# Strassen products for weights times values in the three graph-attention layers of layer 3

## The chip, the cores and the metric

The kernel runs on one core of a Trainium2 chip. The core has five engines, each with its own queue of instructions that it works off in order: TensorE (PE, matrix products into PSUM), VectorE (DVE), ScalarE (ACT), GpSimd (POOL) and SyncE (SP, which here only issues DMAs). Engines wait for each other through semaphores. The metric is the device time of one execution in microseconds (us); lower is better.

## What is computed

A graph of 3327 nodes with 256 features each goes through four residual blocks, `x = layernorm(x + layer(x, adj))`. Layers 0 to 2 are three kinds of masked attention over the adjacency matrix. Layer 3 is a stack of three graph-attention layers, called 3a, 3b and 3c in the kernel:

```python
def _gat_layer(h, adj, W, a):
    Wh = h @ W
    f1 = Wh @ a[:F_out]
    f2 = Wh @ a[F_out:]
    e = leaky_relu(f1 + f2.T, 0.01)
    att = softmax(where(adj > 0, e, NEG_INF), axis=1)
    return elu(att @ Wh)

h = input @ W0
h = _gat_layer(h, adj, W1, a1)
h = _gat_layer(h, adj, W2, a2)
h = _gat_layer(h, adj, W3, a3)
```

All of it is float32. The kernel multiplies the weights by the layer's input first and applies W afterwards (attention is linear in its values), so the large product has shape 3327 x 3327 x 256 in each of the six layers, and the projection is a small product of 256 x 256 per row.

## The kernel before

The nodes are padded to 26 tiles of 128. Queries are worked off in seven blocks: six of 512 queries (four tiles) and a last one of 256 (two tiles). `steps` runs over layers, blocks b and key tiles j; NB is 7 and NT is 26.

For each step `make_weights` builds one tile `e` of unnormalized weights, 128 keys by 512 queries. In the graph-attention layers (`Gat.weights`) that is one ACT instruction, `re` = relu(th * u - rh), and one DVE instruction, `e` = (re + rh) * mask. The vectors `th` and `rh` (one number per key, from `Gat.keys`) and `u` (one per query, from `Gat.block`) hold exponentials, shifted by maxima over all nodes that `Gat.shift` finds so that nothing overflows. The steps are made two to three ahead (LA = 2). There are five buffers for `e` and four for `re`.

PE then multiplies `e` by the values V (256 columns and one column of ones, whose sums norm the weights) into four PSUM banks, the `po` tiles: 257 columns per product, for each key tile and each query tile (L1562). V holds two generations, since the output of one layer is written while the input is read.

Layers 0 (inner blocks) and 2 use Strassen's method instead, over pairs of key tiles: a pair of weight tiles is a 2 x 2 block matrix (two halves of queries, two key tiles), a pair of value tiles another (two key tiles, two halves of features). Seven half-size products take the place of eight. `sums` adds the four combinations of weights (four DVE operations of 128 x 256 per pair, into `ssum`, tag acc with two buffers). `combine` makes the four combinations of values (DVE, once per pair and layer), which go to DRAM (`t_d`) and come back for each block through `fetch_tsum` (256.5 KB each, three buffers, issued on SP). `products` issues the 14 products per pair (L890); `joined` puts the seven results together at the end of a block, on DVE, with one ACT copy.

After a block, `finish` runs as a generator: one piece of it is advanced per step of the next block. In layer 3 before: norm the rows (L1133 to L1137), turn them by a DMA transpose (`turn`: two ACT copies into `planes`, the DMA, two DVE copies, L955), project by W (`projected4`, itself a Strassen product for blocks before the last two, with 12 DVE additions; a plain product, L1174, for the other blocks), elu (L1183, L1186, L1198), a running sum (L1036), and for 3a and 3b the scores of the next layer (L702, two per tile). In 3c the residual and the layer norm follow instead.

The first instructions stand in an order written out by hand (`manual_schedule`, until step 3); after that the framework's scheduler decides how the instructions of an engine follow each other, so the pieces of a finish are interleaved with the weights of the next block. Of tag x4k there are two buffers: the planes and turned rows of a finish, the combinations and, in layer 2, a block's queries (`gT`) share them.

```python
    def strassen(L, b):
        return L.key == "2" or (L.key == "0" and 0 < b < NB - 1)
```

The last block of 3c (`end`) is worked by a path of its own, with the weights kept in V.

Of the kernel before, what the change touches and what calls it, by code (L numbers as in the profile page):

```python
# [8 lines left out]
F32 = mybir.dt.float32  # L9
# [4 lines left out]
AF = mybir.ActivationFunctionType  # L14
ALU = mybir.AluOpType
AX = mybir.AxisListType
# [3 lines left out]
P = 128  # L20
# [4 lines left out]
ALPHA = 0.01  # L25
BETA = 1.0 - ALPHA
# [7 lines left out]
def gnn_stack(ctx: ExitStack, tc: tile.TileContext, a: dict, N: int, out: bass.AP):  # L34
# [8 lines left out]
    nc = tc.nc  # L43
    NT = (N + P - 1) // P
    NP = NT * P
    NB = (NP + CH - 1) // CH
# [36 lines left out]
    n = 8  # L83
# [9 lines left out]
    for k in range(4):  # L93
# [16 lines left out]

    t_d = {
        k: [dram.tile([P, 4 * H + 1], F32, name=f"t{k}_d{p}") for p in range(NT // 2)]
        for k in ("0", "2")
    }
    x_d = {
        k: [dram.tile([P, D], F32, name=f"x{k}_d{t}") for t in range(NT)]
# [478 lines left out]
    def by_pairs(L, b, p):  # L595
        return L.key == "2" and b < NB - 1 and p in (KPAIRS if b > 0 else (5, 7, 8, 10))
# [92 lines left out]
    class Gat:  # L689
# [23 lines left out]
        def shift(self, n):  # L713


            mx = cols.tile([P, 2], F32, tag="mx", name="mx")
            nc.vector.tensor_reduce(mx, self.sd[:, :, :n], AX.X, ALU.max)
            am = cols.tile([P, 2], F32, tag="am", name="am")
            nc.gpsimd.partition_all_reduce(am, mx, P, bass_isa.ReduceOp.max)

            self.nd = cols.tile([P, 1], F32, tag="nd", name="nd")
            self.nc = cols.tile([P, 1], F32, tag="ncs", name="ncs")
            self.ub = cols.tile([P, 1], F32, tag="ub", name="ub")
            nc.vector.tensor_scalar(self.nd, am[:, 1:2], -BETA, None, ALU.mult)
            nc.vector.tensor_tensor(self.nc, am[:, 0:1], am[:, 1:2], ALU.add)
            nc.vector.tensor_scalar(
                self.nc, self.nc, -BETA, 60.0, ALU.mult, ALU.add
            )
            nc.vector.tensor_scalar(self.nc, self.nc, 0.0, None, ALU.min)
            nc.vector.tensor_tensor(self.ub, self.nc, self.nd, ALU.subtract)  # L730

        def keys(self, lo, hi):
            d = self.sd[:, 1, lo:hi]
            nc.scalar.activation(self.th[:, lo:hi], d, AF.Exp, bias=self.nd)
            nc.scalar.activation(
                self.rh[:, lo:hi], d, AF.Exp, bias=self.nc, scale=ALPHA
            )
            nc.vector.tensor_scalar(
                self.nrh[:, lo:hi], self.rh[:, lo:hi], -1.0, None, ALU.mult
            )  # L740
# [10 lines left out]
        def block(self, b):  # L751

            wd = bw(b)
            u = work.tile([P, CH], F32, tag="u", name="u", bufs=2)
            nc.sync.dma_start(
                u[:, :wd], s_d[b].rearrange("o n -> (o n)").partition_broadcast(P)
            )
            for _ in range(6):
                yield
            nc.scalar.activation(  # L760
                u[:, :wd], u[:, :wd], AF.Exp, bias=self.ub, scale=BETA
            )
            self.u[b] = u

# [27 lines left out]


    def strassen(L, b):
        return L.key == "2" or (L.key == "0" and 0 < b < NB - 1)

    tsums = {}

    kept = {("0", 0): 1, ("0", 1): 1, ("0", 2): 1, ("2", NT // 2 - 1): 0}

    def combine(key, p, v, e=None):

# [242 lines left out]
    def finish(L, b, pos):  # L1045
# [5 lines left out]
        wd = bw(b)  # L1051
# [69 lines left out]
                    yield  # L1121
        else:
            p4 = work.tile([P, 4, D], F32, tag="stage", name="p4", bufs=4)
            if L.key == "2":
                z = joined(pos, b, p4)
                nc.vector.tensor_scalar(z, z, TINY, None, ALU.max)
                nc.vector.reciprocal(z, z)
                for k in range(n):
                    nc.scalar.mul(p4[:, k, :], p4[:, k, :], z[:, k : k + 1])
            else:  # L1130
                for k, t in enumerate(ts_):
                    ri = cols.tile([P, 1], F32, tag="ri", name="ri", bufs=4)
                    nc.vector.tensor_scalar(  # L1133
                        ri, pos[k][:, D : D + 1], TINY, None, ALU.max
                    )
                    nc.vector.reciprocal(ri, ri)
                    nc.scalar.mul(p4[:, k, :], pos[k][:, :D], ri)  # L1137
# [10 lines left out]
            if L.key != "2":  # L1148
                pT4 = work.tile([P, 4, 2, P], F32, tag="x4k", name="pT4", bufs=2)
                yield from turn(  # L1150
                    p4,
                    n,
                    lambda t: pT4[:, :n].bitcast(U16).rearrange(
                        "p k h (i t) -> p t k h i", t=2
                    )[:, t],
                    turn_steps(L, b),
                )
                pTs = {k: pT4[:, k] for k in range(n)}
                if b < NB - 2:
                    c4 = work.tile([P, 4, D], F32, tag="x4k", name="c4", bufs=2)  # L1160
                    yield from projected4(pT4, w[L.w], c4)

            def projected(k):


                if L.key == "2":
                    src = p4[:, k, :]
                elif b < NB - 2:
                    src = c4[:, k, :]
                else:  # L1170
                    pm = bank("pproj")
                    pT = pTs.pop(k)
                    for h in range(2):
                        nc.tensor.matmul(  # L1174
                            pm[:, :D],
                            pT[:, h, :],
                            w[L.w][:, h, :],
                            start=(h == 0),
                            stop=(h == 1),
                        )  # L1180
                    src = pm[:, :D]
                e = work.tile([P, D], F32, tag="elu_e", name="elu_e", bufs=2)
                nc.scalar.activation(e, src, AF.Exp)  # L1183
                if L.hidden:
                    y = work.tile([P, D], F32, tag="y", name="z", bufs=6)
                    nc.vector.tensor_scalar(y, src, 0.0, -1.0, ALU.max, ALU.add)  # L1186
                else:
                    y = work.tile([P, D], F32, tag="y", name="y", bufs=6)
                    nc.vector.scalar_tensor_tensor(
                        y, src, 0.0, xr[k], ALU.max, ALU.add  # L1190
                    )
                es[k] = e
                ys.append(y)
# [10 lines left out]
            for p in range(n + 2):  # L1204
                if p >= 2:
                    activated(p - 2)
                    if b == NB - 2:
                        yield
                if 1 <= p <= n:
                    projected(p - 1)  # L1210
                if p > 0:
                    yield
        if not L.hidden:
# [54 lines left out]
            for k in range(0, n, 2):  # L1268
                follow((k, k + 1), dsts)
                yield  # L1270
        if L.gat_next is not None:
            if b == NB - 2:
                yield
                L.gat_next.shift(ts_[-1] + 1)
                yield
                L.gat_next.keys(0, ts_[-1] + 1)
                yield
                if L.key == "0":
                    yield
                    yield  # L1280
            else:
                for _ in range(3):
                    yield
            L.gat_next.rows(b)
        if b == NB - 1:
            for t, x in L.late:
                yield
                L.sum.add(t, x)
            yield
            L.sum.close(nxt[NT - 1])  # L1290
            if L.key == "1":
                yield
                combine("2", NT // 2 - 1, nxt)
            if L.gat_next is not None:
                L.gat_next.keys(ts_[0], NT)

# [126 lines left out]
    def make_weights(L, b, j):  # L1423
        if strassen(L, b) and j % 2 == 0 and kept.get((L.key, j // 2)) != b:
            fetch_tsum(L.key, b, j // 2)
        if L.is_gat:
            made.append(L.gat.weights(b, j))
        elif by_pairs(L, b, j // 2):
            made.append(next(pairs[b, j - j % 2]))
            if j % 2:  # L1430
                e1, e2 = made.pop(), made.pop()
                made.append(None)
                made.append(sums(b, e1, e2))
        else:
            made.append((weights0 if L.key == "0" else weights2)(b, j))
            if strassen(L, b) and j % 2:
                e2, e1 = made.pop(), made.pop()
                made.append(None)
                made.append(sums(b, e1, e2))
# [37 lines left out]
    for s, (L, b, j) in enumerate(steps):  # L1477
# [120 lines left out]
        if nb == NB:  # L1598
            nl, nb = (None if last else layers[L.i + 1]), 0
        begin = 2 if last and b == NB - 2 else 14  # L1600
        if L.is_gat and (b, j) == (0, 22):
            sum_weights(w[L.w])
        if L.key == "2" and b * NT + j in KSTEPS:
            sum_keys(KSTEPS[b * NT + j])
# [90 lines left out]
```

## Time and profile before

| | |
|---|---|
| device time, three runs | 2330.83, 2332.19, 2332.12 us (median 2332.12) |
| span of the profiled execution | 2330.8 us |
| mean granted TensorE clock | 0.998 |
| instructions | 34802 |
| DMA | 214.77 MB, mean 92 GB/s |

The profiled execution is one run; its span is from the first to the last instruction, and equals the shortest of the three times to the precision shown, so little lies around it. In the page's row for DMA queues the one that SP feeds carries 212.28 MB and is busy 28.9% of sixteen engines' time.

By stretches of time (busy us of each engine), layer 2 and then three parts of layer 3:

```profile
900.00:1240.00 340.00, 340.00 (x2125) 288.85 (x2124) 296.74 (x898) 100.87 (x186) 0.00 (x0) 1.00 0.23 71
1735.00:1880.00 145.00, 145.00 (x710) 127.15 (x710) 95.14 (x225) 79.13 (x118) 0.00 (x0) 1.00 0.17 52
2050.00:2195.00 145.00, 145.00 (x708) 127.43 (x708) 96.99 (x232) 78.96 (x115) 0.00 (x0) 1.00 0.23 74
```

The columns are the stretch, its length, then PE, PE's weight loads, DVE, ACT and POOL with their counts of instructions, the granted clock, the DMA share and GB/s. PE is busy without a gap in all; DVE is busy 87% of the time in layer 2 and 66% in layer 3.

### The profile page before, as it was taken

To read this page: it belongs to the slowest core of one execution; us is meant where nothing else is said; L and a number is where in the kernel's file an instruction comes from. 1 tells how busy PE (TensorE), PEld (TensorE's weight loads), DVE (VectorE), ACT (ScalarE), POOL (GpSimd) and SP (SyncE) were. 2 spreads that over 40 slices of the span, in tenths; PEclk is the share of its full clock that TensorE was granted. 3 is DMA by queue.
4 is the path that set the end of the run, shared out by engine and by line. 5 is a ranking of instruction groups with operands and counts; after the bars stand their busy time and mean duration, and the time that the engine had idled before them with its cause. 6 is when DMAs were issued, how large, how long until landed. Compare 5 with 4: busy or idle time off the path is not lost.

```text
span 2330.8 us, 34802 instructions
## 1 busy us (share of the span) xinstructions
PE 2315.7 (99%) x12551; PEld 1975.3 (85%) x12551; DVE 1767.6 (76%) x4877; ACT 1207.5 (52%) x1923; POOL 38.8 (2%) x156
## 2 busy tenths in 40 slices
PE   9999999999999999999999999999999999999997
PEld 7788887888888778888888988888888888888887
DVE  7789999867777778889889876666656666666676
ACT  4677777765555422233323355555655555655553
POOL 0000001000000000000000000000000000000000
PEclk9999999999999999999999999999999999999999
DMA  8655565422222322213212321210211111132111
GB/s 278 192 188 183 173 193 188 150 82 80 75 70 72 100 55 89 80 46 93 75 51 83 107 84 55 70 52 27 77 48 44 46 58 53 44 100 70 62 45 46
DMA packets 147297, 214.77 MB, mean 92 GB/s; under 512 B 76093, under 2 KB 101172, under 8 KB 142516
## 3 DMA queue, kind: packets, MB, share of 16 engines
q1 hardware_dynamic: 146852, 212.28, 28.9%
q8 instruction: 99, 1.62, 0.3%
q14 instruction: 74, 0.61, 0.1%
q10 hardware_dynamic: 272, 0.26, 0.0%
HBM read 167.53 MB, written 28.19 MB: 84 GB/s over the span
## 4 chain that ended last, share of the span: by engine, by line
PE 98%; DVE 1%; DMA 0%; ACT 0%; issue 0%; SPq 0%; DVEq 0%; ACTq 0%
PE po L1562 52%; PE po L890 20%; PE ps L635 6%; PE ps L499 6%; PE ps L674 5%; PE pproj L1001 3%; PE po L1527 1%; PE pv L1255 1%; PE pgq L529 1%; PE pproj L1174 1%; PE pk L359 0%; PE pq L323 0%; DMA stage<-in_adj_a 0%; PE pn L335 0%; PE pr L175 0%; PE turned L80 0%
## 5 line engine op out<-in xcount | busy, mean ns | idle before, releaser
L1562 PE MATMUL po<-v,e 128*128 128x257 f32 x5616 | 1247.7, 381 | 0.1
L1562 PEld LDWEIGHTS po<-v,e 128*128 128x128 f32 x5616 | 1058.0, 190 | 163.2 <-issue 9.3
L768 ACT ACTIVATE re<-u,nrh,th 128x512 f32<-128x512 f32 (+1 forms) x728 | 555.7, 780 | 493.9 <-DVE e L779 488.4
L779 DVE SCALAR_TENSOR_TENSOR e<-re,rh,mask 128x512 f32<-128x512 f32 (+1 forms) x702 | 501.9, 718 | 340.4 <-PE po L1562 314.7
L890 PE MATMUL po<-tsums,ssum 128*128 128x128 f32 (+1 forms) x1794 | 250.5, 275 | 0.0
L890 PEld LDWEIGHTS po<-tsums,ssum 128*128 128x128 f32 x1794 | 225.5, 192 | 1.1 <-ACT y L1093 0.3
L890 PEld LDWEIGHTS po<-v,e 128*128 128x128 f32 x1196 | 172.7, 191 | 37.6 <-issue 24.1
L890 PE MATMUL po<-v,e 128*128 128x129 f32 x1196 | 185.9, 275 | 0.0
L512 ACT ACTIVATE ex<-ps,rq 128x512 f32<-128x512 f32 (+1 forms) x183 | 118.9, 652 | 115.2 <-PE ps L499 112.4
L484 DVE SCALAR_TENSOR_TENSOR e<-ex,mask 128x512 f32<-128x512 f32 (+1 forms) x182 | 115.6, 650 | 48.3 <-ACT ex L648 24.8
L513 DVE SCALAR_TENSOR_TENSOR e<-ex,mask 128x512 f32<-128x512 f32 (+1 forms) x183 | 117.2, 646 | 33.4 <-ACT ex L512 32.9
L499 PE MATMUL ps<-ft,ft 128*128 128x512 f32 (+1 forms) x312 | 142.5, 561 | 0.0
L648 ACT ACTIVATE ex<-ex,off 128x512 f32<-128x512 f32 x98 | 67.5, 717 | 132.0 <-DVE ex L664 94.4
L674 PE MATMUL ps<-gT,ft 128*128 128x512 f32 (+1 forms) x336 | 129.8, 527 | 0.0
L455 DVE CUSTOM_DVE_ANT_0 acc<-acc,stage 128x1024 uint16<-128x1024 uint16 (+1 forms) x168 | 109.0, 649 | 11.7 <-DMA stage<-in_adj_a 8.6
L682 ACT ACTIVATE ex<-ps,off 128x512 f32<-128x512 f32 (+1 forms) x84 | 51.8, 620 | 101.3 <-PE ps L674 100.1
L674 PEld LDWEIGHTS ps<-gT,ft 128*128 128x128 f32 x336 | 61.2, 190 | 44.5 <-issue 38.5
L890 PE MATMUL po<-tsums,e 128*128 128x128 f32 x598 | 92.2, 275 | 0.4 <-DVE c L1100 0.4
L890 PE MATMUL po<-v,ssum 128*128 128x128 f32 x598 | 92.3, 275 | 0.0
L442 ACT ACTIVATE mask<-pos 128x1024 uint8<-128x1024 bf16 (+1 forms) x87 | 86.4, 993 | 2.1
L441 ACT ACTIVATE pos<-stage 128x1024 bf16<-128x1024 int32 (+1 forms) x87 | 85.6, 983 | 0.0
L890 PEld LDWEIGHTS po<-tsums,e 128*128 128x128 f32 x598 | 79.3, 192 | 0.6 <-issue 0.6
(322 smaller groups left out, 2432.6 us busy)
## 6 DMA issues: line engine op xcount, KB each, us to landing
mask<-mask_d SPq DMA_DIRECT2D x30, 1664.0 KB
stage<-in_adj_a SPq DMA_DIRECT2D x78, 512.0 KB
tsums<-t_d SPq DMA_DIRECT2D x152, 256.5 KB
mask_d<-mask SPq DMA_DIRECT2D x6, 1664.0 KB
u<-s_d SPq DMA_DIRECT2D x24, 256.0 KB
xT<-in_xT SPq DMA_DIRECT2D x10, 512.0 KB
mask<-mask_d SPq DMA_DIRECT2D x5, 832.0 KB
t_d<-tsums SPq DMA_DIRECT2D x14, 256.5 KB
```

What stands on the lines that cost most here:

```text
L442: nc.scalar.activation(mask(b, j, 2), t_[:, : 2 * wd], AF.Sign)
L455: nc.vector.tensor_tensor(acc, acc, st[:, h * wd : (h + 1) * wd], ALU.add)
L484: nc.vector.scalar_tensor_tensor(e[:, :wd], t_[:, :wd], 0.0, mask(b, j), ALU.add, ALU.mult)
L499: nc.tensor.matmul(ps[:, :wd], FT[j // 4][:, 0, (j % 4) * P : (j % 4 + 1) * P], FT[b][:, 1, :wd], start=True, stop=True,)
L512: nc.scalar.activation(t_[:, c], ps[:, c], AF.Exp, scale=rq[:, j : j + 1])
L513: nc.vector.scalar_tensor_tensor(e[:, c], t_[:, c], 0.0, mask(b, j)[:, c], ALU.add, ALU.mult)
L635: nc.tensor.matmul(ps[:, i * D : (i + 1) * D], l, r, start=True, stop=True)
L674: nc.tensor.matmul(ps[:, :wd], FT[j // 4][:, h, (j % 4) * P : (j % 4 + 1) * P], g[:, h, :wd], start=(h == 0), stop=(h == 1),)
L768: nc.scalar.activation(t_[:, :wd], self.u[b][:, :wd], AF.Relu, bias=self.nrh[:, j : j + 1], scale=self.th[:, j : j + 1],)
L779: nc.vector.scalar_tensor_tensor(e[:, :wd], t_[:, :wd], self.rh[:, j : j + 1], mask(b, j), ALU.add, ALU.mult,)
L890: nc.tensor.matmul(o, x, y, start=(p == 0 and g not in banks[:i]), stop=(p == NT // 2 - 1 and g not in banks[i + 1 :]),)
L1562: nc.tensor.matmul(pos[k], e[:, k * P : (k + 1) * P], V[L.i % 2][i], start=(i == 0), stop=(i == NT - 1),)
```

## The change

Layer 3 takes the Strassen path: 3a and 3b in all seven blocks, 3c in all but the last. The combinations of values for it are made in the finish of the layer before (two pairs per block, the last pair at the end of the layer) and written to three new sets of DRAM tiles. The finish of a block in layer 3 begins with `joined`. The projection in layer 3 becomes plain in all blocks; layer 1 keeps the Strassen one. The weights of a graph-attention layer (layer 1 too) are shifted per query instead of by one common maximum, so that sums and differences of them stay in range; `shift` finds the minimum of the query scores beside the maximum of the key scores for that.

```diff
     t_d = {
         k: [dram.tile([P, 4 * H + 1], F32, name=f"t{k}_d{p}") for p in range(NT // 2)]
-        for k in ("0", "2")
+        for k in ("0", "2", "3a", "3b", "3c")
     }
...
             nc.vector.tensor_reduce(mx, self.sd[:, :, :n], AX.X, ALU.max)
+            lo = cols.tile([P, 1], F32, tag="lo", name="lo")
+            nc.vector.tensor_reduce(lo, self.sd[:, 0, :n], AX.X, ALU.min)
+            nc.vector.tensor_scalar(mx[:, 0:1], lo, -1.0, None, ALU.mult)
...
-            nc.vector.tensor_scalar(self.nd, am[:, 1:2], -BETA, None, ALU.mult)
-            nc.vector.tensor_tensor(self.nc, am[:, 0:1], am[:, 1:2], ALU.add)
-            nc.vector.tensor_scalar(
-                self.nc, self.nc, -BETA, 60.0, ALU.mult, ALU.add
-            )
-            nc.vector.tensor_scalar(self.nc, self.nc, 0.0, None, ALU.min)
-            nc.vector.tensor_tensor(self.ub, self.nc, self.nd, ALU.subtract)
+            nc.vector.tensor_tensor(self.nc, am[:, 1:2], am[:, 0:1], ALU.subtract)
+            nc.vector.tensor_scalar(self.nc, self.nc, BETA, 0.0, ALU.mult, ALU.min)
+            nc.vector.tensor_tensor(self.nc, self.nc, am[:, 1:2], ALU.subtract)
+            nc.vector.tensor_scalar(self.nc, self.nc, 60.0, None, ALU.add)
+            nc.vector.tensor_scalar(self.ub, am[:, 0:1], -BETA, None, ALU.mult)
+            nc.vector.tensor_tensor(self.nd, self.nc, self.ub, ALU.subtract)
...
     def strassen(L, b):
-        return L.key == "2" or (L.key == "0" and 0 < b < NB - 1)
+        if L.key == "0":
+            return 0 < b < NB - 1
+        if L.key == "3c":
+            return b < NB - 1
+        return L.key != "1"
...
-    kept = {("0", 0): 1, ("0", 1): 1, ("0", 2): 1, ("2", NT // 2 - 1): 0}
+    kept = {("0", 0): 1, ("0", 1): 1, ("0", 2): 1}
+    kept.update({(key, NT // 2 - 1): 0 for key in ("2", "3a", "3b", "3c")})
...
-            if L.key == "2":
+            if strassen(L, b):
                 z = joined(pos, b, p4)
...
-                if b < NB - 2:
+                if L.key == "1" and b < NB - 2:
                     c4 = work.tile([P, 4, D], F32, tag="x4k", name="c4", bufs=2)
                     yield from projected4(pT4, w[L.w], c4)
...
+                    if L.hidden and p % 2 and b < NB - 1:
+                        combine(layers[L.i + 1].key, (ts_[0] + p - 3) // 2, nxt)
...
             for k in range(0, n, 2):
                 follow((k, k + 1), dsts)
                 yield
+                if L.key == "2" and b < NB - 1:
+                    combine("3a", (ts_[0] + k) // 2, nxt)
...
-            if L.key == "1":
+            if L.i:
                 yield
-                combine("2", NT // 2 - 1, nxt)
+                combine(layers[L.i + 1].key, NT // 2 - 1, nxt)
...
-        if L.is_gat:
-            made.append(L.gat.weights(b, j))
-        elif by_pairs(L, b, j // 2):
+        if by_pairs(L, b, j // 2):
...
-            made.append((weights0 if L.key == "0" else weights2)(b, j))
+            if L.is_gat:
+                made.append(L.gat.weights(b, j))
+            else:
+                made.append((weights0 if L.key == "0" else weights2)(b, j))
             if strassen(L, b) and j % 2:
...
-        if L.is_gat and (b, j) == (0, 22):
+        if L.key == "1" and (b, j) == (0, 22):
             sum_weights(w[L.w])
```

The arguments of the exponentials in `Gat.keys` and `Gat.block` change with the shift (which of them has the factor 0.01, and a sign); their number stays.

## The prediction

> **What bounds the kernel now.** I read the page's busy times first, then the chain of waits, then the groups of instructions in layer 3, then the timeline of the vector engine (DVE). Page, busy times:
>
> ```profile
> PE 2315.7 (99%) x12551; PEld 1975.3 (85%) x12551; DVE 1767.6 (76%) x4877; ACT 1207.5 (52%) x1923; POOL 38.8 (2%) x156
> PE 98%; DVE 1%; DMA 0%; ACT 0%; issue 0%; SPq 0%; DVEq 0%; ACTq 0%
> ```
>
> TensorE is full, and the chain that ended last (second line) is 98% PE. The chain between 1720 and 1880 us shows one whole block of layer 3:
>
> ```profile
> 1767.46 26.22 PE po L1562 x120
> 1793.68 1.78 PE pproj L1001 x16
> 1795.46 1.74 PE po L1562 x8
> 1797.20 0.89 PE pproj L1001 x8
> 1798.09 1.74 PE po L1562 x8
> 1799.83 0.44 PE pproj L1001 x4
> 1800.27 15.60 PE po L1562 x72
> 1815.87 0.11 PE psr L746
> ```
>
> These sum to 48.5 us per block with no gap. A float32 matmul shows as two records; of 257 columns a record takes 15.60/72 = 216.7 ns. What Strassen's products take is in the chain of layers 0 and 2, where one pair of key tiles is 28 records, 3.12 us:
>
> ```profile
> 1241.79 3.12 PE po L890 x28
> ```
>
> Groups by form, 1735 to 1880 us (three blocks), then 900 to 1240 us (layer 2):
>
> ```profile
> L779 DVE SCALAR_TENSOR_TENSOR e<-re,rh,mask 128x512 f32<-128x512 f32 x78 | 58.2, 750 | 45.1 <-PE po L1562 42.0 <-PE psr L746 2.9
> L955 DVE COPY pT<-turned 128x1024 uint16<-128x1024 uint16 x6 | 4.1, 741 | 0.0
> ...
> L841 DVE TENSOR_TENSOR ssum<-e,ssum 128x256 f32<-128x256 f32 x52 | 21.9, 422 | 0.4
> ```
>
> In layer 3 the DVE waits for PE before its masks (45.1 of 145 us). That idle time is the room for the new work. The timeline of the DVE, 1005 to 1008 us, shows what an operation really occupies:
>
> ```profile
> 1005.86 0.42 DVE L840 TENSOR_TENSOR ssum<-ssum,e 128x256 f32<-128x256 f32 x1
> 1006.20 0.42 DVE L655 TENSOR_TENSOR ex<-ex,ps 128x256 f32<-128x256 f32 x1
> 1006.53 0.42 DVE L841 TENSOR_TENSOR ssum<-e,ssum 128x256 f32<-128x256 f32 x1
> 1006.86 0.42 DVE L656 TENSOR_TENSOR ex<-ex,ps 128x256 f32<-128x256 f32 x1
> ```
>
> It lasts 0.42 us but the next starts after 0.335. I price by these start-to-start steps wherever the DVE is never idle: 0.335 for 128x256, 0.20 for 128x128 (0.28 to 0.29 long), 0.662 for a layer-3 mask of 512 (0.75 long), 0.395 for one of 256, 0.345 for a score (L702), 0.64 for a turned copy, 0.08 for a column. Busy shares, which add up the long durations, overstate DVE load.
>
> **What the Trainium skill says.** "Perfetto Trace Analysis", section Identifying the Most-Contended Engine, warns that matmul busy share does not show how near PE is to its limit; here the chain, gapless and 98% PE, settles it. "VectorE: DVE Perf Modes", section The perf-mode tier table: `tensor_tensor` on float32 runs in the 1× mode, one element a cycle; at the page's 0.96 GHz that is 267 ns for 256; the trace agrees with 335 (68 fixed). Section The DRAIN you can't avoid says the next operation waits until the pipe is empty; the trace differs, overlapping 85 of 420 ns, and decides. "TensorE: Matmul & The Clock Gate", section What's actually happening: an idle window of about 3.4 us halves PE's clock. PE is never idle so long here (granted clock 0.998), so no run shows it.
>
> **The change, part by part.**
>
> *PE, removed.* A pair of key tiles was 16 records, 3.467 us; it becomes 28 records, 3.12 us: 0.347 less. Of a whole block's 13 pairs: 4.5 us. The half block (last, two query tiles) goes from 13 x 1.733 to 13 x 1.56: 2.25. There are 18 whole blocks (3a, 3b and 3c have six each), and two half blocks that change: 81.2 + 4.5 = 85.7 us. *PE, added.* Plain projections: 16 records of 256 columns, 3.47, for 28 of 128, 3.12: 0.35 more in 15 blocks, 5.2. Net on PE: -80.5 us, a whole block 44.1 instead of 48.5.
>
> *DVE, added and removed, per whole block of 3a or 3b,* counted in the instruction list of the changed program: 26 masks x 0.662 = 17.2; sums, 52 x 0.335 = 17.4 (new); joining the products, 2.9 (new, in place of eight columns, 0.6); turned copies 1.3; relu, elu and mean, 12 x 0.335 = 4.0; scores 8 x 0.345 = 2.8; combinations of values for the next layer, 8 x 0.20 = 1.6 (new). The 12 additions of the Strassen projection (4.0) go; relu now reads PSUM, 0.335 for 0.205. Sum 47.2, before about 29.5. So **DVE passes PE: 47.2 against 44.1**. In 3c, with no scores or combinations but with the layer norm: 44.3. Half block: 33.7 (it carries the finish of the whole block before) against 23.8 on PE. First blocks: 43.6 in 3a (PE 40.6), 41.7 in 3b and 3c (PE 42.3).
>
> *How it falls within a block.* With two sum buffers (tag acc) the DVE starts pair k's sums only when PE has done pair k-2, so it can be about 2.5 us ahead, no more. A plain pair is 2.66 us on DVE and 3.12 on PE: it gains 0.46 per pair. The list has two bursts: at the second pair the joining (6.2 us of DVE for one pair of PE work), and at the sixth and seventh relu, scores and combinations (together 13.4 to 13.7 us, against two pairs and the projections on PE, 9.7). The first uses up the lead (2.5 + 3.1 - 6.2: about 0.6 unhidden); the four pairs after it give back about 0.8, so of the second burst's 3.8 about 3.1 stay open; the six last pairs restore the lead. Whole block of 3a, 3b: 44.1 + 3.7 = 47.8. In 3c the second burst is smaller (5.4 to 5.8 and 2.9, then 3.1 and 4.7): 44.1 + about 0.7.
>
> *Waits that come with it.* The turn chain (scaled rows, planes, DMA transpose, pT) starts after the joining. From its last operation: four scalings 1.9, one `re` 0.8, two plane copies 2.0, the transpose 3.66 (the chain of waits shows DMA turned<-planes so once, at 776.95): 8.4 us; in the list the DVE has 7 masks and 10 sums before pT, 8.0. So about 0.4 us of wait a block, bounded below by 0 (PE-paced stretch) and above by 1.5 (on SP the transpose stands behind a fetch of combined values that waits for PE). Behind the waiting pT copies stand the next sums and masks, for which PE waits. The new fetches (256.5 KB a pair) go out when PE has done pair k-3 and are needed two pairs, 6.2 us, later; a fetch of layer 2 lands some 2.3 us after its issue, so I cost them at nothing; behind the 1664 KB mask the cover is 9 us against about 7. Combining for 3a in layer 2 adds 1.6 us of DVE to blocks of 85.5 us where PE is the limit: 0, at most 1 a block. The new shift is a few columns per layer: 0. Semaphore hops between ACT, DVE and PE: I take 0.6 a block in 3c, where slack is thin.
>
> *Sum.* 3a and 3b, ten whole blocks: 47.8 + 0.4 against 48.5: -3. 3c, five: 44.8 + 0.4 + 0.6 = 45.8: -13.5. Half blocks: 33.7 less the lead of 2.5 = 31.2 against about 29.5 (the starts of their finishing rows): +3.4. First blocks: +1 each in 3b and 3c (the tail of the half block's finish), 0 in 3a: +2. The tail: the fifth block of 3c now joins before it turns, 2.3 late: +2.3. Total about -8.8. The profiled span is 2330.8 us; the median of the runs shown, 2332.1, is 1.3 above, and the lowest is equal to the span. 2330.8 - 8.8 + 1.3 = **2323 us**. Of 80 us taken from PE, 72 are given to the DVE.
>
> **The rivals.**
> - *PE stays the limit:* the DVE's new work fits in its idle time. For it: 45 of 145 us idle before the masks. Against: 47.2 over 44.1, and a lead of one pair. 2332 - 80 = 2252 us. Chance 0.06.
> - *The turn chain decides (slower):* the DVE, now the limiting engine, stands at the pT copies for the DMA transpose. Price: each 0.4 us in 17 blocks is 7 us. From 0.9 us of wait a block the gain is gone; at the bound of 1.5 it is +19 on the forecast, 2342; own range 2337 to 2360. For it: 8.4 against 8.0, and PE-dependent fetches ahead of the transpose on SP. Against: the stretch before pT has no other finishing work, so part of the wait falls on DVE time that PE's pace leaves free. Chance 0.30.
> - *PE's clock drops:* gaps in PE add up to an idle window, and 3.4 us at half clock cost 1.7 in each of 17 blocks: 2353. Against: the open 3.1 us come in pieces between single products. Chance 0.05.
> - *Layer 2 gives it back:* the second combination of a block waits for the first one's DMA, since the query block holds the other buffer of tag x4k; 1 us in six blocks: 2330. Chance 0.10.
>
> **How the numbers follow.** The forecast has 0.49, own range 2310 to 2334. A measurement here tells 0.2%, 4.7 us. Faster by more: 0.43 of the forecast's case, plus 0.06: 0.49. Within: 0.06 of it, 0.09 of the layer 2 case, 0.05 of the turn case: 0.20. Slower: 0.31. The range to hold eight in ten: low 2300 (DVE steps 1% shorter and leads fully used), high 2350 (the upper bound of the turn wait and some of the others).
>
> **What would show it.** Right: PE busy falls in layer 3 and its idle time is put down to DVE e and ssum; DVE is near full there; whole blocks take about 48 us in 3a and 3b and 46 in 3c; the chain of waits alternates PE and DVE. Wrong: blocks of 44 us (PE still the limit), of 50 and more with DVE idle before pT on turned<-planes (turn chain), or a granted clock below 0.99.

## The result, and the profile after

The changed kernel takes 2340.9 us (median of five, 2337.6 to 2344.2) against 2331.9 (2330.8 to 2332.2) for the kernel before: ratio 1.004, 95% interval 1.0027 to 1.0052. It is slower by 0.4%, where 2323 and a gain were forecast. The profiled execution spans 2339.1 us, before 2330.8. (Its own time is 2340.9. In every run here whose span is on record the time lies 1.7 to 2.2 us above it, so some 2 us do lie around a span, before too.) The page's busy times and its DVE row of slices:

```profile
PE 2274.8 (97%) x15335; PEld 2017.4 (86%) x15335; DVE 2072.2 (89%) x6032; ACT 1206.9 (52%) x1928; POOL 53.2 (2%) x195
...
DVE  7789999867777778899889899999999999999997
```

PE's busy time fell by 41 us, and the DVE row is nines from the 24th slice to the last but one: the vector engine is full through layer 3. The chain of waits breaks off in this trace (its shares add up to 18% of the span), so I read windows. Columns are PE, PEld, DVE, ACT and POOL busy, the granted clock, the DMA share and GB/s. One whole block of 3b and one of 3c, before:

```profile
1730.50:1779.00 48.50, 48.50 (x239) 42.53 (x237) 31.73 (x76) 26.50 (x40) 0.00 (x0) 1.00 0.17 52
2095.20:2143.60 48.40, 48.40 (x237) 42.54 (x236) 32.38 (x78) 26.39 (x39) 0.00 (x0) 1.00 0.23 73
```

and after, with the half blocks of 3a and 3b (third and fourth line):

```profile
1738.00:1786.00 48.00, 44.30 (x374) 43.11 (x373) 47.10 (x126) 27.25 (x40) 1.34 (x2) 1.00 0.46 140
2110.00:2157.00 47.00, 45.48 (x384) 44.47 (x384) 45.39 (x127) 26.09 (x38) 0.00 (x0) 1.00 0.52 150
...
1660.00:1695.80 35.80, 31.15 (x205) 27.46 (x204) 33.16 (x133) 22.03 (x42) 0.71 (x3) 0.95 0.63 181
...
1979.80:2017.80 38.00, 31.89 (x214) 28.19 (x215) 33.24 (x133) 22.45 (x41) 0.71 (x3) 0.96 0.59 173
```

In the whole blocks PE went from never idle to 3.7 us (3b) and 1.5 us (3c) idle, while DVE went from two thirds busy to full: the limit has changed engines, as forecast. The half blocks are where the two kernels part most. Cutting the span at the first row scaling on ACT (p<-p,zs after, p<-po,ri before) of each block's finish gives the whole account:

| stretch | before | after | forecast change | measured |
|---|---|---|---|---|
| layer 2, up to its half block's finish | 466.1 | 468.5 | 0 | +2.4 |
| first block of 3a, and the tail | 42.0 + 41.0 | 45.8 + 38.9 | +2.3 | +1.7 |
| 3a, five whole blocks | 243.2 | 240.3 | -1.5 | -2.9 |
| half block of 3a, first of 3b | 74.2 | 81.3 | +2.7 | +7.1 |
| 3b, five whole blocks | 242.2 | 238.6 | -1.5 | -3.6 |
| half block of 3b, first of 3c | 74.2 | 83.1 | +2.7 | +8.9 |
| 3c, five whole blocks | 242.6 | 237.3 | -13.5 | -5.3 |

The sum is +8.4 (before rounding) where -8.8 was forecast (layers 0 and 1 differ by 0.1). The miss of 17.2 us lies in the half blocks (10.6 over the forecast), in 3c (8.2) and in layer 2 (2.4). The whole blocks of 3a and 3b did 3.5 better, and the first block of 3a with the tail 0.6. (These two share a row because the first scaling comes later in a block that is joined first.)

What ends a half block shows in the waits of the one in 3b, 1979.8 to 2017.8 (engine, line, what it waited for: us in total, times, longest):

```profile
PE po L897 <- DVE ssum L847: 2.7, 2, 2.3
DVE zs L929 <- ACT p L923: 2.7, 1, 2.7
ACT u L762 <- DMA u<-s_d: 2.6, 1, 2.6
...
PE po L897 <- DMA tsums<-t3b_d: 1.6, 2, 1.4
```

and in the timeline of DVE and ACT there (start, length, engine, line, operation; in brackets the idle time before it):

```profile
2008.29 0.28 DVE L846 TENSOR_TENSOR ssum<-e 128x128 f32<-128x128 f32 x1
...
2010.13 0.72 ACT L762 ACTIVATE u<-u,ub 128x512 f32<-128x512 f32 x1 [2.56 <-DMA u<-s_d]
...
2010.96 0.24 ACT L923 COPY p<-po 128x128 f32<-128x128 f32 x1
...
2011.24 0.16 DVE L929 COPY zs<-po 128x1 f32<-128x1 f32 x1 [2.66 <-ACT p L923]
2011.31 0.28 DVE L847 TENSOR_TENSOR ssum<-ssum,e 128x128 f32<-128x128 f32 x1
```

At the end of the block the DVE stands 2.66 us at the joining. Its row-sum copy (`zs`) starts when ACT's copy of M1 (the first of the seven products, `p<-po`) is out of PSUM, and that copy stands behind the exponential of a `u` of the next layer, for whose DMA ACT waits 2.56 us. Behind the waiting `zs` stand the block's own last two sums, for which PE waits 2.3 us. In 3a's half block the same hole is 2.05 us.

### The profile page after: what moved, and what is told of

It is laid out like the page before. It is cut to its first block, busy times and chain, and to the rows that moved or that the text cites. A ratio compares the mean times of both kernels' runs of the same rounds, so it can differ in the third digit from the quotient of the medians.

```text
span 2339.1 us, 42193 instructions
## 1 busy us (share of the span) xinstructions
PE 2274.8 (97%) x15335; PEld 2017.4 (86%) x15335; DVE 2072.2 (89%) x6032; ACT 1206.9 (52%) x1928; POOL 53.2 (2%) x195
## 5 line engine op out<-in xcount | busy, mean ns | idle before, releaser
L897 PE MATMUL po<-tsums,ssum 128*128 128x128 f32 (+1 forms) x4758 | 677.8, 278 | 13.9 <-DVE ssum L847 5.1
L897 PEld LDWEIGHTS po<-tsums,ssum 128*128 128x128 f32 x4758 | 605.3, 193 | 24.1 <-DVE ssum L847 7.6
L897 PE MATMUL po<-v,e 128*128 128x129 f32 x3172 | 503.1, 278 | 16.4 <-DVE e L781 15.1
L897 PEld LDWEIGHTS po<-v,e 128*128 128x128 f32 x3172 | 440.2, 192 | 64.0 <-issue 25.6
L1574 PE MATMUL po<-v,e 128*128 128x257 f32 x1664 | 376.0, 381 | 0.1
L1574 PEld LDWEIGHTS po<-v,e 128*128 128x128 f32 x1664 | 313.9, 190 | 53.9 <-issue 9.3
L897 PE MATMUL po<-tsums,e 128*128 128x128 f32 x1586 | 248.4, 276 | 0.0
L897 PEld LDWEIGHTS po<-v,ssum 128*128 128x128 f32 x1586 | 210.7, 192 | 1.2 <-DVE ssum L848 0.8
L845 DVE TENSOR_TENSOR ssum<-e 128x256 f32<-128x256 f32 (+1 forms) x416 | 167.4, 403 | 4.4 <-PE po L897 1.8
L848 DVE TENSOR_TENSOR ssum<-e,ssum 128x256 f32<-128x256 f32 (+1 forms) x416 | 168.1, 404 | 1.5
L847 DVE TENSOR_TENSOR ssum<-ssum,e 128x256 f32<-128x256 f32 (+1 forms) x416 | 167.7, 403 | 1.4
L846 DVE TENSOR_TENSOR ssum<-e 128x256 f32<-128x256 f32 (+1 forms) x416 | 167.5, 403 | 0.5
```

Of the source, the lines that this page charges most:

```text
L845: nc.vector.tensor_tensor(s3, e11, e21, ALU.subtract)
L846: nc.vector.tensor_tensor(s1, e21, e22, ALU.add)
L847: nc.vector.tensor_tensor(s2, s1, e11, ALU.subtract)
L848: nc.vector.tensor_tensor(s4, e12, s2, ALU.subtract)
L897: nc.tensor.matmul(o, x, y, start=(p == 0 and g not in banks[:i]), stop=(p == NT // 2 - 1 and g not in banks[i + 1 :]),)
L1574: nc.tensor.matmul(pos[k], e[:, k * P : (k + 1) * P], V[L.i % 2][i], start=(i == 0), stop=(i == NT - 1),)
```

## The experiments

Each is told beside the kernel before on the same chip (2331.1 to 2332.0 us). "Block times" are the distances of the row scalings, as in the table.

**Plain half blocks** (e1).

```diff
-        if L.key == "3c":
+        if L.is_gat and L.key != "1":
             return b < NB - 1
```

> The half blocks of 3a and 3b are multiplied plainly again, the rest of the change stays. Theory A (in a half block the vector engine is the limit, with no lead to use, so the 52 sums of 128x128 stand in the time in full): half blocks of 35.8 and 38.0 us go back to about 29.6 each, and the time from 2340.9 to about 2326. Theory B (the turn chain or the fetches set the half block, not the sums): both stay in it, PE gets 2.2 us of products a half block more, and the time is 2338 to 2345.

Measured: 2315.3 us, ratio 0.9938 (0.9925 to 0.9950): 25.6 us less than the changed kernel, and faster than before. Windows of 3a's half block and 3b's first:

```profile
1661.00:1687.90 26.90, 25.89 (x122) 21.44 (x121) 20.74 (x73) 17.97 (x35) 1.87 (x3) 1.00 0.35 78
1687.90:1734.40 46.50, 45.85 (x397) 45.15 (x396) 46.38 (x123) 27.78 (x43) 0.10 (x1) 1.00 0.50 143
```

The pair takes 73.4 us (73.2 at the next change of layer) for 81.3 and 83.1. So the two Strassen half blocks cost 17.8 us: theory A, with more gained than its 2326. A further 5.1 us came in 3c, whose five blocks took 232.2 for 237.3, and 3.4 in the tail (35.5 for 38.9), though nothing was changed there; e5 explains them.

**Strassen in 3c alone** (e4): `strassen` false in 3a and 3b, Strassen's projection kept there, no combinations for them.

> Strassen in layer 3c alone; 3a and 3b are as in the kernel before (plain products, Strassen projection), layer 2 makes no combinations for 3a, and 3b makes those for 3c. Theory A (the loss is made in 3a's and 3b's half blocks and in layer 2, 3c by itself gains): about 2325 (2332 less the 7.6 us that 3c's interior and tail show). Theory B (3c's gain is paid back by what comes with it, such as fetches and turn waits): 2330 to 2335.

2320.5 us, 0.9954 (0.9941 to 0.9966). Layer 2's blocks are 85.5 us again (86.0, 85.5 and 86.0 after) and 3c's interior blocks 45.1 to 46.0: theory A, with a larger gain (10.9 us) than its 7.6. The five blocks of 3c and the tail took 232.0 and 35.7 us, about as in e1.

**Plain half blocks and 3a plain altogether** (e8).

> Plain half blocks, and layer 3a plain altogether (as before, with Strassen's projection; layer 2 makes no combinations). Theory A (3a's Strassen blocks win nothing net: 3 us lost in layer 2 and 1.5 in 3a against 3 won in its half block, by the block times of the two kernels): 2313 to 2316. Theory B (3a wins as 3b does, 3.5 us): 2318 to 2320.

2314.6 us, 0.9928 (0.9915 to 0.9940), as theory A had it: beside e1's 2315.3, Strassen in 3a is worth nothing. By the block times of the two kernels it saves 1.4 us in the whole of 3a and costs 3.2 in layer 2, where the combinations for it are made.

**Two of four sums left out** (e6). In layer 3 the products take unsummed quarters of the weights in place of the sums s2 and s4, and the row sums are enlarged so that the values stay small; the output is another function. (A first form, e3, without the enlarged sums, has no time.)

> Left out in layer 3: two of the four sums of a pair of key tiles (s2 and s4; the products take unsummed weights in their place), with the row sums enlarged so that the values stay small; PE's stream is the same, and the vector engine has 26 operations, 8.7 us, less in a whole block and 5.2 us less in a half block. Theory vector work (its load sets the blocks of 3a and 3b): whole blocks fall to about 45 us in all three, half blocks by 5 us, and the time by 40 to 55 us, to 2286 to 2301. Theory turn chain: less work ahead of pT means a longer wait there (about 3 us in place of 1 to 1.6), a block gains 2 us at most, and the time stays above 2310.

2305.0 us, 0.9887 (0.9871 to 0.9902), 36 us less than the changed kernel: below the turn chain's bound, above the range of the load theory. Of the 5.2 us of work taken out of each half block only 1.6 and 3.9 come back in it (34.2 and 34.1 us for 35.8 and 38.0). The DVE's busy time there fell from 33.2 and 33.3 us to 29.2 and 29.0, and its pauses grew from 2.6 and 4.8 to 5.0 and 5.1. A hole of 1.95 us stands at 3a's joining here too, but the trace puts it down to PE's products and not to ACT. So the load is a limit of the half block, and not the only one. The whole blocks of 3b tell more:

```profile
1777.00:1824.00 47.00, 44.96 (x382) 43.81 (x381) 40.08 (x106) 26.53 (x40) 1.36 (x2) 1.00 0.48 138
```

With 8.7 us less on DVE the blocks are only 1.1 shorter (46.8 for 47.9 on average). DVE now has 7 us free, yet PE idles 2 us: by its gaps in this block 1.1 us at the masks behind the scores and 0.6 at the projections. The load was one limit; by these gaps the burst of finishing work in the middle of the block is another right behind it, which no run tried alone. In 3c, without scores and combinations, blocks fell to 45.0.

**The pT copies two key tiles later** (e2: `else 4` to `else 6` in turn_steps).

> The copies into pT of layer 3 stand two key tiles later in the order (6 steps in place of 4), so the vector engine has 2.7 us more of masks and sums ahead of them. Theory turn wait: the vector engine's idle time before pT in layer 3 (20.4 us in 15 blocks) is lost time; it goes, and the time falls by 8 to 13 us, to 2328 to 2333. Theory vector work: the engine is the limit of the block anyway and the wait only moves to another place in it; the time stays within 4 us of 2341.

2342.9 us, 1.0045 (1.0029 to 1.0060), and the wait before pT is unchanged (19.9 us against 20.4). By the trace the edit didn't do what it says: in the whole blocks the DVE still has 6 masks and 11 sums between the joining and pT, where it had 6 or 7 and 10 or 11, since the scheduler sets the order. Only in the first blocks of 3b and 3c did the copies move (6 masks and 14 sums for 4 and 10), and there their wait went (1.2 and 0.8 us before). So e2 decides nothing about the turn wait in whole blocks; neither theory is shown by it.

**128 PE instructions more at the start** (e5).

```diff
+    for _ in range(32):
+        nc.tensor.matmul(turned[:1, :1], ones[:, :1], ones[:, :1], start=True, stop=True)
```

> The changed kernel with 32 matrix products of one element added at its very start (128 PE instructions), nothing else. In 3c of the changed kernel each DMA transpose of the turned rows takes 3.5 to 3.9 us and a 16 KB packet of the instruction queue falls into it; with plain half blocks it takes 2.6 us and none falls into it. Theory collision (the number of instructions issued before sets when the fetch comes): the fetch moves by half its period, 3c's transposes take 2.6 us, its whole blocks 45.7 us in place of 46.7, and the time is 3 to 5 us lower less up to 3 us for the added products, 2336 to 2340; transposes elsewhere may be hit in their place. Theory half block (the half block's own order of DMAs makes 3c slow): 3c's blocks stay at 46.7 and the time at 2341 to 2344.

2343.1 us, 1.0045 (1.0033 to 1.0058), but 3c did what the collision theory says. In the changed kernel, DVE timeline and then the DMA queues from 2115.8 to 2119.5 (packets, MB, share of 16 engines):

```profile
2117.94 0.42 DVE L846 TENSOR_TENSOR ssum<-e 128x256 f32<-128x256 f32 x1
2119.97 1.36 DVE L962 COPY pT<-turned 128x1024 uint16<-128x1024 uint16 x2 [1.61 <-DMA turned<-planes]
```

```profile
q1 hardware_dynamic: 2111, 0.59, 124.2%
q8 instruction: 1, 0.02, 1.6%
```

In e5 the same place of the same block:

```profile
2126.92 0.42 DVE L848 TENSOR_TENSOR ssum<-e 128x256 f32<-128x256 f32 x1
2128.03 1.36 DVE L964 COPY pT<-turned 128x1024 uint16<-128x1024 uint16 x2 [0.69 <-DMA turned<-planes]
```

A single packet of 16 KB of the instruction queue, 0.96 us long, falls into the transpose, whose 2048 packets then take 3.50 us from first to last start, and 2.60 in e5 without it. In the changed kernel a packet falls into the first four whole blocks' transposes of 3c (3.5 to 3.9 us) and just ahead of the fifth (3.0); in e5 and e1 into or close to none of them (2.59 to 2.60), and the five blocks take 232.2 and 232.3 us for 237.3. The tail is shorter too, 35.7 us for 38.9: in the changed kernel a packet falls onto the end of its transpose, the DVE waits 1.99 us there for pT (0.34 in e5), and a drop of PE's clock follows. These 8.2 us were not kept. Up to layer 2 the kernel lost 6.0 us, where up to 3 were expected for the added instructions, and the five blocks of 3b took 244.4 us for 238.6, the first of them 51.6. A drop of PE's clock (1747 us, 1.7 us of PE) falls into that one, and the waits before pT in 3b were 0.7 to 2.1 us for 0.4 to 0.9; the rest of these losses was not traced. So the collision is shown as the cause in 3c and the tail (the half blocks are not shorter: 37.5 and 37.2 us for 35.8 and 38.0), while the total stays where the other theory had it.

**Layer 3's fetches of combined values from POOL's queue** (e9; `nc.gpsimd.dma_start` in fetch_tsum).

> The changed kernel, with layer 3's fetches of combined values issued by POOL in place of SP, so that the transpose of the turned rows, the row of scores and the broadcast u no longer stand behind a fetch that waits for PE. Theory queue (in the half blocks SP's order makes the chain at the change of layer late: transposes go out 0.5 and 2.2 us after their planes are ready, ACT waits 2.6 us for u and the vector engine 2.1 and 2.7 us behind it): half blocks fall from 35.8 and 38.0 us by 2 to 4 us each, and the time by 4 to 8 us, to 2333 to 2337. Theory vector work: half blocks stay within 1 us, and the time at 2338 to 2344.

2356.7 us, 1.0123 (1.0105 to 1.0142), outside both ranges. The transposes no longer stand behind such a fetch, but most take 5.5 us or more from issue to pT in place of 4.4, and the waits before pT in layer 3 add up to 33.8 us for 20.4. Half blocks of 36.0 and 37.4 us keep a hole of 2.34 us in 3a and 1.80 in 3b, now at the next layer's `nrh` (`rh` with its sign changed); ACT still waits 2.5 and 2.0 us there for the DMA of a u. e12, the same edit on e7 below:

> As the kernel with plain half blocks and the pT copies and relu on ACT (2295), with the fetches of combined values issued by POOL. Theory queue: with plain half blocks SP has nothing to hold up (its transposes go out at once there), so nothing is gained: 2293 to 2297. If fetches that go out late cost time in whole blocks too, up to 5 us less, 2290.

2313.6 us for 2295.1, outside both ranges: 18.5 us lost. In its trace PE stands 24.6 us before the projections for ACT's copy into pT, 13.7 in e7, and the transposes of most whole blocks take 5.4 to 5.9 us from issue to pT, 4.3 to 4.4 in most of e7's. So PE's wait there grew by 11 us; the rest of the 18.5 was not traced. (A POOL issue takes about 540 ns, one on SP 320; whether that matters was not tried.)

**Three buffers for u** (e10), so that the fetch whose exponential blocks ACT goes out earlier.

> The changed kernel with three buffers for the broadcast rows u in place of two (room made by one buffer less of xsum and mrow in another tag), so that the fetch of u for the next layer's second block need not wait for the last weights of the half block. Theory hole (at the end of a half block the vector engine stands 2.05 and 2.66 us behind ACT's copy out of PSUM, and ACT behind the exponential of that u): the hole goes, the half blocks fall by about 2 us each to 34 and 36, the time to 2335 to 2338. Theory load (the vector engine's work fills the half block, the hole only shows its end): half blocks and time stay within 1 us and 3 us.

2343.2 us, 1.0047 (1.0034 to 1.0060). Half blocks 35.8 and 36.3: the first as theory load has it, the second 1.7 shorter, near what theory hole has; the time is within theory load's 3 us. By the trace the edit is no test of the wait for u. ACT no longer waits for the second u, but with the third buffer the exponential of a third stands ahead of the weights, and ACT waits for its DMA:

```profile
1686.58 0.72 ACT L762 ACTIVATE u<-u,ub 128x512 f32<-128x512 f32 x1 [1.29 <-DMA u<-s_d]
...
1688.04 1.46 DVE L781 SCALAR_TENSOR_TENSOR e<-re,rh,mask 128x512 f32<-128x512 f32 x2 [1.48 <-ACT re L770]
```

So the DVE now stands before the next layer's first masks, 1.48 us here and 1.95 in 3b. e13, the same beside plain half blocks and e7's edits:

> As the kernel with plain half blocks and the pT copies and relu on ACT (2295), with three buffers for u. Theory hole: there ACT waits 12.6 us in all for u, and where weights stand behind it PE may wait too: up to 5 us less, 2290. If that wait falls on ACT's free time: 2293 to 2297.

2307.0 us, 12 more than without: its half blocks take 29.6 and 28.8 us for 26.1 and 26.0. Neither value was expected. The trace shows the same at the change of layer, in 3a:

```profile
1678.42 0.72 ACT L762 ACTIVATE u<-u,ub 128x512 f32<-128x512 f32 x1 [2.79 <-DMA u<-s_d]
...
1679.88 0.75 DVE L781 SCALAR_TENSOR_TENSOR e<-re,rh,mask 128x512 f32<-128x512 f32 x1 [4.04 <-ACT re L770]
```

The DVE stands 4.04 us (3.28 in 3b) before the masks where it stood 0.94 in e7, because a third exponential waits for its DMA ahead of the weights. No kernel here puts such an exponential behind them, which would test the hole.

**Work moved from DVE to ACT, with plain half blocks** (e7, the fastest).

```diff
-                nc.scalar.activation(e, src, AF.Exp)
                 if L.hidden:
-                    nc.vector.tensor_scalar(y, src, 0.0, -1.0, ALU.max, ALU.add)
+                    nc.scalar.activation(e, src, AF.Relu, scale=-1.0)
+                    nc.scalar.activation(e, e, AF.Exp, scale=-1.0)
+                    y = src
...
-                nc.vector.scalar_tensor_tensor(x, e, 1.0, y, ALU.min, ALU.add)
+                    nc.vector.scalar_tensor_tensor(x, e, -1.0, y, ALU.add, ALU.max)
...
-            nc.vector.tensor_copy(out(t), trv[:, t])
+            (copy or nc.vector.tensor_copy)(out(t), trv[:, t])
```

(`copy` is `nc.scalar.copy` in layer 3 for b < NB - 2.)

> Plain half blocks, and in layer 3's whole blocks two things moved from the vector engine to ACT: the copies of the turned rows into pT (1.3 us a block), and in 3a and 3b the relu of elu (1.3 us a block; ACT computes exp(-relu(-x)), the vector engine the larger of that less 1 and x). Theory vector work: whole blocks of 3a and 3b fall from 47.7 to about 45.3 us and those of 3c from 45.7 to about 45, together 25 to 30 us below the 2315 of plain half blocks: 2285 to 2292. Theory turn chain: the wait for the transpose is now ACT's, the weights behind it come late, and blocks gain less than 1 us: 2305 or more.

2295.1 us, 0.9845 (0.9831 to 0.9858): 1.55% faster than before and 20 us faster than e1. Of the 25 to 30 us of theory vector work that is most, and well past the other's bound. Windows of 46.0 us in 3b and 45.5 in 3c:

```profile
1771.00:1817.00 46.00, 44.91 (x382) 44.06 (x381) 44.69 (x125) 29.70 (x46) 0.20 (x2) 1.00 0.50 141
2122.00:2167.50 45.50, 44.75 (x384) 44.07 (x383) 44.44 (x123) 28.27 (x41) 0.00 (x0) 1.00 0.51 154
```

PE is 98% busy again and DVE 97 to 98%: both are near full. PE idles only at the projections, which wait for pT (1.1 us in the first window, 0.75 in the second).

**The same edits with Strassen half blocks** (e15).

> The changed kernel, Strassen half blocks included, with the pT copies of whole blocks and the relu of elu on ACT. Theory: the whole blocks gain as they did beside plain half blocks (20 us), and the half blocks keep most of their 16 to 20 us of loss, since what ends them is the chain to the next layer's weights and not the vector engine's load: half blocks of 34 us or more, time 2312 to 2320. Theory vector work: the half blocks shrink too, by the 2.7 us taken from the vector engine there and more, to 31 us or less, time below 2308.

2316.9 us, 0.9938 (0.9925 to 0.9950), inside the first theory's range: whole blocks of 46 us in 3a and 3b as in e7, half blocks of 36.1 and 35.6 with holes of 2.39 and 3.15 us. Beside e7 the time is 22 us longer, 17.0 of them in the half blocks and what follows each: about the 17.8 of e1, so that price does not shrink when whole blocks are relieved.

**pT two tiles later on e7** (e14): 2301.4 us, 0.9877 (0.9862 to 0.9892), slower than e7 and above both ranges; as in e2 the scheduler left about as much work ahead of pT as in e7 (in most blocks 7 or 8 masks and 11 to 13 sums), so this too is no test of the wait.

> As the kernel with plain half blocks and the pT copies and relu on ACT (2295), with the pT copies two key tiles later in the order, as was tried on the changed kernel. Theory: the wait at the turned rows costs only while PE is the limit; here PE stands 15.5 us in 18 blocks before its projections for pT, and these 10 to 13 us go: 2282 to 2286. Theory order (the scheduler and the transfers only move the wait, as in the changed kernel, where two key tiles later gave nothing): 2292 to 2298.

**Combinations for layer 3 on POOL, on e7** (e11).

> As the kernel with plain half blocks and the pT copies and relu on ACT (2295), with the combinations of values for layer 3 computed on POOL in place of the vector engine (1.6 us of its work per block in layer 2, 3a and 3b). Theory vector work: layer 2's blocks go back from 85.6 to 86.0 us to 85.5 and those of 3a and 3b from 46.1 to 45.2, together 10 us: 2284 to 2288. Theory port: POOL and the vector engine get in each other's way, and operations of the vector engine lengthen; the time is 2293 or more.

2329.6 us, 0.9991 (0.9985 to 0.9998), 34 us slower than e7. Groups by form in 3b, 1735 to 1880 us, with e7's line for the scores after e11's:

```profile
L702 DVE CUSTOM_DVE_ANT_0 ejunk<-v,row_3c 128x256 f32<-128x256 f32 x24 | 12.9, 574 | 0.0
...
L824 POOL TENSOR_TENSOR tsum<-v,v 128x128 f32<-128x128 f32 x6 | 4.4, 738 | 7.3 <-DVE v L1209 7.3
```

```profile
L702 DVE CUSTOM_DVE_ANT_0 ejunk<-v,row_3c 128x256 f32<-128x256 f32 x30 | 11.5, 420 | 0.0
```

POOL needs 738 ns where the DVE needs 290, and the DVE's scores beside it lengthen from 420 to 574 ns. The Trainium skill, "GPSIMD Engine Reference", section Key points, says that POOL shares its SBUF interfaces with the vector engine, and names contention with operations that have two inputs in SBUF; these have, and the trace agrees. The ten whole blocks of 3a and 3b lost 14.9 us in all. About as much, 15.4 us, was lost at the changes of layer: the first blocks of 3b and 3c took 55.5 and 57.2 us for 46.3, the half blocks ahead of them 2.3 less each. In 3b's first block the DVE stands 2.6 us for the maximum that POOL finds in `shift`, whose queue now holds the combinations too, and PE stands 6.6 us; that this is the cause was not tried. Layer 2 kept its loss although its additions for 3a were off the DVE.

## Why the prediction was wrong

*Right.* The DVE passes PE. The whole blocks of 3a and 3b were forecast at 48.2 and took 47.9 on average; the load was forecast at 47.2, and the window above has the DVE 47.1 of 48.0 us busy. The first blocks of 3b and 3c, forecast one us longer, took 0.9 and 0.4 longer (45.5 and 45.0 for 44.5 and 44.6). The new shift cost nothing that shows in layer 1.

*The step that failed: "Half blocks: 33.7 less the lead of 2.5 = 31.2".* They took 35.8 and 38.0. The load was sized well: the DVE was busy 33.2 and 33.3 us. The lead was the error, and the end of the block, which the sum put at nothing. A lead of 2.5 us would have left the DVE 31.2 us of work in the stretch; it had all but 0.5 of its 33.7, and stood idle 2.6 and 4.8 us besides. In 3a these are 2.05 at the joining, 0.3 at pT and 0.25 at the shift; in 3b 2.66, 0.7 and 0.25 at the same places and 1.1 at ssum, while PE waits 1.4 for a fetched combination. e1 shows the price of Strassen there, 17.8 us with what follows; e6 that taking work away shortens the half block, but not by all of that work. What the hole at the joining alone costs stays open: in e9 and e10 ACT still waited for a u there.

*3c: the turn wait of 0.4 us was mis-sized.* It was 1.06 to 2.38 us in the five whole blocks that follow the first, 8.4 in all where the sum has 2.0, and in four of them above the 1.5 that was taken for its upper bound. Two terms: the chain from issue to pT takes 4.3 us even undisturbed, not the 3.66 read from one place in the chain of waits, which leaves a wait of 0.65 (e1, e5); the rest is the instruction fetch in the transpose, about 1 us a block, which the sum did not have (e5). That e1's undisturbed blocks, 45.7 us, agree with the forecast's 45.8 is luck. One of them:

```profile
2097.10:2142.80 45.70, 45.03 (x382) 44.03 (x381) 45.05 (x125) 26.05 (x39) 0.00 (x0) 1.00 0.52 154
```

The DVE is busy 45.05 us, not the 44.3 of the sum, and its only pause is the 0.65 before pT; so its load and this wait make up the block, and the 0.7 for the bursts and 0.6 for hops between engines are not seen beside them. The sum also priced five blocks alike. The last, which was 48.9 before, took 49.6, and 49.2 in e1 and e5: it gained nothing from Strassen there, and counting it at 45.8 was 3.4 to 3.8 us of the 8.2. With two sums left out (e6) it took 45.1.

*Layer 2: "0, at most 1 a block".* 2.4 us were lost, 0.1 to 0.6 a block and 1.0 in the last stretch: inside that bound, but the sum had 0. Where nothing is combined for 3a the blocks take 85.5 us again (e4, e8). In the changed kernel's layer 2 the DVE waits at the first addition of a combination (view of line L822 in that layer: what its engine waited for, us, times):

```profile
  DMA t3a_d<-tsum: 1.4, 2
```

That is the wait of the rival "layer 2 gives it back": the buffer waits for the former combination's DMA. One wait (0.39 us) stands in a block that took 0.56 more than before, the other (0.98) in the last stretch, which took 0.96 more; a third stretch, 0.52 longer, has none. So making the combinations is shown as the cause, and this wait as a part of it only by its place; the rest stays open. That the additions themselves are not the rest is not shown by e11, since there the DVE's scores in layer 2 lengthened from 417 to 498 ns beside POOL's additions.

*PE's clock* (the rival with 0.05) did drop, three times in layer 3 before the tail and once in it: 3.4 us at half, 1.7 us of PE each. In 1 us windows of the change from 3a to 3b:

```profile
1688.00:1689.00 1.00, 0.00 (x0) 0.00 (x0) 0.00 (x0) 0.93 (x3) 0.00 (x0) 1.00 0.97 345
1689.00:1690.00 1.00, 0.41 (x2) 0.30 (x2) 0.82 (x6) 1.00 (x3) 0.00 (x0) 1.00 1.28 466
1690.00:1691.00 1.00, 0.74 (x5) 0.52 (x5) 1.00 (x2) 1.00 (x2) 0.00 (x0) 1.00 0.93 386
...
1692.00:1693.00 1.00, 1.00 (x5) 1.00 (x6) 1.00 (x6) 1.00 (x2) 0.00 (x0) 0.50 0.97 413
1693.00:1694.00 1.00, 1.00 (x6) 1.00 (x6) 1.00 (x4) 0.39 (x1) 0.00 (x0) 0.50 0.75 293
```

Two drops follow the holes of the half blocks; the DVE had no pause between the hole and the end of either stretch, so there the drop is not seen to add to it. The one at 1442 us lies in the 49.5 us block of 3a, where its neighbours took 47.6 to 48.3; but that block was 1.0 us longer than its neighbours before as well. The fourth lies in the tail, behind the wait that e5 removes.

*The turn chain*, the slower rival, gave the measured number (2342), but not for its reason: that is luck. In the whole blocks of 3a and 3b the wait before pT was 0.4 to 0.9 us, 0.7 on average for the 0.4 of the sum, and 11 of the 20 us in layer 3 lie in 3c. No kernel put the copies behind more work in the whole blocks of 3a and 3b, so what the wait costs there is open.

*Small sums.* 48.5 less 4.5 and plus 0.35 is 44.3, not 44.1; PE was busy 44.8 to 45.0 us in whole blocks of 3c (e1, e7). The 0.8 that four pairs give back is not worked out: four times 0.46 is 1.8. The clock rival comes to 2352, not 2353. The 267 ns for 256 elements is an estimate from the clock that the page states; the price that was used, 335, is the trace's.

## What to carry to other kernels

When a change moves the limit to another engine, price each stretch by what begins and ends it: here a lead between engines was worth little in the last and smaller block of a layer, which ends in a chain of waits. Apply the change only to the blocks in which the old limit had the more to give; here plain half blocks alone turned +0.4% into -0.6%, and two small pieces of work moved to an engine that was half idle made it -1.55%. And read in the trace where a moved instruction really stands, and what its engine now waits for, before an experiment on it is believed: in e2, e10 and e14 the edit left the wait that it was to remove.

## What the runs showed of the hardware

- Instruction fetches are DMA traffic too: a 16 KB packet takes about 0.96 us and stretches a transpose of 2048 packets of 256 bytes from 2.6 us to 3.5 to 3.9. In 3c, whose blocks have nearly equal counts of instructions, the collision repeated in four blocks running, and 128 instructions far ahead shifted it away.
- PE's clock was halved for 3.4 us after an idle gap of 1.65 us followed by two partly idle us. In the 3.4 us before the four drops PE was busy 35, 54, 34 and 38% of the time; the longest gaps in them were 0.67, 1.65, 2.26 and 2.12 us. The Trainium skill, "TensorE: Matmul & The Clock Gate", section What's actually happening, speaks of an idle window of about 3.4 us; shorter idle time was enough here.
- The five runs of the changed kernel differ by 6.6 us (mean granted clock 0.993 to 0.995), those of the kernel before by 1.4 (0.998 in its profiled execution). Why was not tried.
